# Two layers of graph attention: all products of the slots in four 64 by 64 tiles of TensorE

## The chip, the cores and the metric

The kernel runs on one core of a Trainium2 chip. The metric is the device time of one execution in microseconds. Shown are the median of three runs, and one further execution that the hardware profiler recorded.

## The reference, cut to what matters

Two layers on `x` of shape (8, 2048, 256), float32, with one adjacency matrix of 2048 by 2048 and four heads of 64.

```python
# layer 0: attention in chunks of 256 keys, each with its own softmax, summed over the chunks
q, k, v = (x @ Wq.T + bq, x @ Wk.T + bk, x @ Wv.T + bv)        # each split into 4 heads of 64
scores = clip(einsum('bhnd,bhjcd->bhnjc', q, kc) / 8, -10, 10)  # j: 8 chunks, c: 256 keys
scores = where(mask == 0, -10, scores)
ctx = einsum('bhnjc,bhjcd->bhnd', softmax(scores, -1), vc)
out = layernorm(ctx @ Wo.T + bo + x) * gamma + beta
x = layernorm(x + out)
# layer 1: graph attention
Wh = x @ W                                                      # 4 heads of 64
e = leaky_relu(s_src[:, :, None, :] + s_dst[:, None, :, :], 0.2)
alpha = softmax(where(adj != 0, e, -inf), axis=2)
x = layernorm(x + elu(einsum('bijh,bjhd->bihd', alpha, Wh)))
```

## The kernel before, in words

The eight batches follow one another. Layer 0 of batch b runs beside layer 1 of batch b - 1 (`lower`), so that the first batch has layer 0 alone and a last stretch has layer 1 alone. The order of the work is written out by hand: a manual schedule keeps every engine's program order, and tables give the step at which each side job is issued.

**Layer 0 runs in slots**, 64 per batch. A slot is 512 queries (`q`), a pair of heads (`hp`) and a chunk of 256 keys (`c`), in two tiles of 128 keys (`u`). In the loop over `s` (lines 934 to 999) the program issues, in this order: the slab of mask limits for slot s + 3 (`load_slab`); the side job of the table "ahead"; `normalize(s - 1)`; `scores(s + 1)`; side jobs "beside"; the first half of `product(s)`; the exponentials of slot s + 1 on ScalarE; a step of layer 1; the second half of `product(s)`; the jobs "behind".
- `scores` (L375) makes four products `ps` of 64 (one head's width) by 128 keys by 512 queries; the two heads of a pair lie in the upper and lower 64 partitions, so these are two row tiles, 64\*128. VectorE then clips and masks each `ps` of 128 by 1024 into `pr` (L396).
- `product` (L411) takes `pr` as weights, 128 keys by 64 queries, against `vaug`, 128 keys by 64 values and a one for the denominator. Outputs go to the upper or lower 64 partitions of `pc`, so these are two column tiles, 128\*64. ScalarE copies each `pc` to `raw` (L429).
- `normalize` takes the reciprocal (VectorE) and multiplies and adds on GpSimd.

**Layer 1 (`Layer1`)** works on units of a head and 1024 nodes (`BANKS = (8, 8)`), each over 16 tiles of 128 neighbours. `make` (L741, VectorE) forms a tile `e` of 128 by 1024 from a row `srow`, a column `gd` and a mask `et`; `use` (L763, TensorE) multiplies it with `waug` in two column tiles, 128\*64, summing a unit in two banks `pa`. Two tiles are made and used per slot; the ring of `e` has three buffers, and `make` is two tiles ahead.

**Side jobs.** `Between` does the output projection (`po`, L537), two layer norms, and layer 1's input product (`pw`, L581) of a group of 512 nodes; `Closing` does the last layer norm; `project` makes keys, queries (`pp`, L329) and values (`pv`, L345) for the next batch between slot 63 and slot 0 (the list `order`, L1028); `factors` (`fs`) makes layer 1's exponentials there. All of these use TensorE as 128\*128.

**PSUM**[...]: two pairs that `two_banks` gives out in turn (`psA`: `ps`, `pp`, `pv`, large `po` and `pw`), one `psC` for `pc`, two `psL` for `pa` and small things, and one `psM` for `po`, `pw` of few rows, `context` and `factors`.

A float32 matmul of the program stands in the trace as two pairs of LDWEIGHTS and MATMUL; these are called records below.

Of the kernel before, what the change touches and what calls it, by code (L numbers as in the profile page):

```python
# [8 lines left out]
F32 = mybir.dt.float32  # L9
# [13 lines left out]
def adj_resnorm_kernel(  # L23
# [35 lines left out]
    BANKS = (8, 8)  # L59
# [4 lines left out]
    QS = HP * NK  # L64
    SLOTS = NCH * QS
    UNITS = [(m, h) for m in range(len(BANKS)) for h in range(H)]
    FIRST = [sum(BANKS[:m]) for m in range(len(BANKS))]
    TILES = len(UNITS) * NT
    STEP = TILES // SLOTS
    LATE = 14  # L70
    WIDE = max(BANKS)
    JG = 2
    AHEAD_E = 3
    n_banks = WIDE // QT
    assert TILES == STEP * SLOTS and NT % JG == 0 and all(n == WIDE for n in BANKS)

# [5 lines left out]
    edges = ctx.enter_context(tc.tile_pool(name="edges", bufs=4))  # L82
# [5 lines left out]
    psM = ctx.enter_context(tc.tile_pool(name="psM", bufs=1, space=bass.MemoryType.PSUM))  # L88
# [30 lines left out]
    vaug = big.tile([P, NT, H, D1], F32, tag="vaug", name="vaug")  # L119

    clipD = [tc.dram_tile([P, NT, CH], I8, name=f"clipD{q}") for q in range(NCH)]
    edgeD = [tc.dram_tile([P, NT, n * P], U8, name=f"edgeD{m}") for m, n in enumerate(BANKS)]
# [36 lines left out]
    w1_sb = consts.tile([P, KC, F + 2 * H], F32, tag="w1_sb", name="w1_sb")  # L159
    nc.scalar.dma_start(out=w1_sb[:, :, :F], in_=w1.rearrange("(c p) f -> p c f", p=P))  # L160
# [10 lines left out]
    def finish_constants():  # L171
        for k, a_sb in enumerate(aa):
            for c in range(KC):
                wa = small.tile([P, F], F32, tag="ee", name="wa")
                nc.vector.tensor_mul(wa, w1_sb[:, c, :F], a_sb)
                nc.vector.tensor_reduce(
                    w1_sb[:, c, F + k * H : F + (k + 1) * H],
                    wa.rearrange("p (h d) -> p h d", h=H),
                    AX.X,
                    ALU.add,  # L180
                )


        pb0 = psM.tile([P, CH], F32, tag="psM", name="pb0")
# [22 lines left out]
    class Masks:  # L207
# [34 lines left out]
        def turn(self, t, m, ab):  # L242
# [11 lines left out]

            def stores():
                nc.sync.dma_start(
                    out=clipD[q][:, j0 : j0 + n, u * P : (u + 1) * P], in_=clip[:, :n]
                )
                nc.sync.dma_start(out=edgeD[mi][:, j0 : j0 + n, at : at + P], in_=edge[:, :n])
# [46 lines left out]
    def project(b, g):  # L306
# [34 lines left out]
        def values():  # L341
            pv = two_banks([P, QT, F], "pv")
            for u in range(QT):
                for kc in range(KC):
                    nc.tensor.matmul(  # L345
                        pv[:, u, :],
                        lhsT=st["xT"][:, kc, u * P : (u + 1) * P],
                        rhs=wv_sb[:, kc, :],
                        start=(kc == 0),
                        stop=(kc == KC - 1),  # L350
                    )
            nc.scalar.copy(
                vaug[:, QT * g : QT * (g + 1), :, :D],
                pv.rearrange("p t (h d) -> p t h d", h=H),
            )
# [9 lines left out]

    where = [(s // QS, s % QS // NK, s % NK) for s in range(SLOTS)]
    slab_of, probs, raws, accs = {}, {}, {}, {}

    def load_slab(s):
        q, hp, c = where[s]  # L370
        slab = slabs.tile([P, KT, CH], I8, tag="slab", name="slab")
        nc.sync.dma_start(out=slab, in_=clipD[q][:, KT * c : KT * (c + 1), :])
        slab_of[s] = slab

    def scores(s):  # L375
        q, hp, c = where[s]
        slab = slab_of.pop(s)
        cols = slice(q * CH, (q + 1) * CH)
        pss = []
        for u in range(KT):  # L380
            t = KT * c + u
            ps = two_banks([P, 2, CH], "ps")
            for k in range(2):
                rows = slice(k * D, (k + 1) * D)
                nc.tensor.matmul(  # L385
                    ps[:, k, :],
                    lhsT=kT[rows, hp, t * P : (t + 1) * P],
                    rhs=qT[rows, hp, cols],
                    start=True,
                    stop=True,  # L390
                )
            pss.append(ps)
# [17 lines left out]
    def product(s, k, alone):  # L410
        q, hp, c = where[s]  # L411
        if k == 0:
            raws[s] = small.tile([P, 2, QT, D1], F32, tag="raw", name="raw")

        if alone and k:
            pc = one_bank([P, QT, D1], "pc")
        else:
            pc = psC.tile([P, QT, D1], F32, tag="psC", name="pc")
        for i in range(QT):
            for u in range(KT):  # L420
                for z in range(2):
                    nc.tensor.matmul(  # L422
                        pc[z * D : (z + 1) * D, i, :],
                        lhsT=probs[s][u][:, k, i * P + z * D : i * P + (z + 1) * D],
                        rhs=vaug[:, KT * c + u, 2 * hp + k, :],
                        start=(u == 0),
                        stop=(u == KT - 1),
                    )
        nc.scalar.copy(raws[s][:, k], pc)  # L429

    def normalize(s):

        q, hp, c = where[s]
        raw = raws.pop(s)
        del probs[s]
        rd = small.tile([P, 2, QT, 1], F32, tag="rd", name="rd")
        nc.vector.reciprocal(rd, raw[:, :, :, D:D1])  # L437
        if c == 0:
            accs[q, hp] = small.tile([P, QT, 2, D], F32, tag="acc", name="acc")
        accv = accs[q, hp].rearrange("p t k d -> p k t d")  # L440
        part = accv
        if c:
            part = small.tile([P, 2, QT, D], F32, tag="part", name="part", bufs=1)
        nc.gpsimd.tensor_mul(part, raw[:, :, :, :D], rd.to_broadcast([P, 2, QT, D]))  # L444
        if c:
            nc.gpsimd.tensor_add(accv, accv, part)  # L446
# [3 lines left out]
    def send_context(b, q, hp):  # L450
        acc = accs.pop((q, hp))
        cols = slice(hp * P, (hp + 1) * P)
        nc.scalar.dma_start(
            out=by_node(ctxD, b, q)[:, :, cols], in_=acc.rearrange("p t k d -> p t (k d)")
        )

    def load_context(b, q, hp):
        t = small.tile([P, 1, CH], F32, tag="ctx", name="ctx", bufs=1)
        load_squares(t, ctxD[b, q * CH : (q + 1) * CH, hp * P : (hp + 1) * P])
        sums[q, hp] = t  # L460

    def turn_context(q, hp):

        nc.vector.transpose(qT[:, hp, q * CH : (q + 1) * CH], sums.pop((q, hp))[:, 0, :])  # L464

    def context(q, hp):
        acc = accs.pop((q, hp))
        pt = psM.tile([P, CH], F32, tag="psM", name="pt")
        for i in range(QT):
            nc.tensor.transpose(  # L470
                pt[:, i * P : (i + 1) * P], acc[:, i].rearrange("p k d -> p (k d)"), identf
            )
        nc.scalar.copy(qT[:, hp, q * CH : (q + 1) * CH], pt)
# [37 lines left out]
    class Between:  # L511
# [16 lines left out]
        def output(self, us):  # L528
            n = len(us)
            if n == QT:  # L530
                po = two_banks([P, QT, F], "po")
            else:
                po = psM.tile([P, 2, F], F32, tag="psM", name="po")
# [39 lines left out]
        def values(self, us):  # L573
            n, t = len(us), QT * self.g + us[0]
            if n == 1:
                pw = psM.tile([P, 1, CH], F32, tag="psM", name="pw")
            else:
                pw = two_banks([P, 2, CH], "pw")
            for k, u in enumerate(us):
                for c in range(KC):  # L580
                    nc.tensor.matmul(  # L581
                        pw[:, k, : F + 2 * H],
                        lhsT=self.x1T[:, c, u * P : (u + 1) * P],
                        rhs=w1_sb[:, c, :],
                        start=(c == 0),
                        stop=(c == KC - 1),
                    )
            nc.scalar.copy(
                self.waug[:, t : t + n, :, :D],
                pw[:, :, :F].rearrange("p k (h d) -> p k h d", h=H),  # L590
            )
            nc.scalar.copy(
                self.sd[:, :, t : t + n], pw[:, :, F : F + 2 * H].rearrange("p k x -> p x k")
            )
# [3 lines left out]
    AHEAD = {12: lambda o: o.load()}  # L598
    BESIDE = {
        1: [lambda o: o.bias()],  # L600
        4: [lambda o: o.add((0, 1))],
        5: [lambda o: o.add((2, 3)), lambda o: o.a.stats((0, 1))],
# [17 lines left out]
        4: [lambda o: o.add((0, 1))],  # L620
        5: [lambda o: o.add((2, 3))],
# [21 lines left out]
    def factors(b, sd, waug):  # L643
# [3 lines left out]
        s, d = sd[:, :H, :], sd[:, H:, :]  # L647
        top = small.tile([P, H], F32, tag="top", name="top")
        topb = top.unsqueeze(2).to_broadcast([P, H, NT])
        ed = small.tile([P, H, NT], F32, tag="ed", name="ed", bufs=1)  # L650
        gd = small.tile([P, H, NT], F32, tag="gd", name="gd")
        st = {}

        def most():
            nc.vector.tensor_reduce(top, d, AX.X, ALU.max)
            pt = psM.tile([P, CH], F32, tag="psM", name="pt")
            nc.tensor.transpose(pt[:H, :P], top, identf)
            st["most"] = small.tile([H, 1], F32, tag="most", name="most")
            nc.vector.tensor_reduce(st["most"], pt[:H, :P], AX.X, ALU.max)
# [446 lines left out]
```

## Time and profile before

| | us |
|---|---|
| median of 3 runs | 3774.59 (3774.26 to 3775.82) |
| profiled execution, its time | 3776.29 |
| profiled execution, its span | 3774.5 |
| TensorE matmul busy | 3664.0 (97% of the span) |
| VectorE busy | 3133.7 (83%) |
| ScalarE busy | 1988.0 (53%) |
| GpSimd busy | 1365.5 (36%) |

Engines are PE (TensorE's matmuls), PEld (its weight loads, which run beside matmuls), DVE (VectorE), ACT (ScalarE), POOL (GpSimd) and SPq (the queue of SyncE, from which most transfers are issued). A row of the profile names line, engine, operation, output and inputs, the shapes, the count, busy time and the mean of one in ns. The part after the last bar is the time that the engine sat idle before these instructions, and what ended it. "issue" means that the engine waited for nothing that the profile shows.

### The profile page before, as it was taken

The page shows a single profiled execution, that of the slowest core. Times are in us where ns is not written, and L with a number is a line of the kernel's source. Part 1 is how long each engine was busy: PE and PEld are TensorE (multiplying, and loading weights), DVE is VectorE, ACT ScalarE, POOL GpSimd, SP SyncE. Part 2 cuts the span into 40 slices and gives each one's busy share as a digit, 9 for nine tenths or more (in the row PEclk, how much of TensorE's full clock was granted, in tenths as well). Part 3 has the DMA queues.
Part 4 walks back from the last instruction along what each step waited for, and adds up shares of the span by engine and source line. Part 5 has one row for each costly group of instructions (what it writes and reads, how often), then busy time and mean ns, then how long its engine had stood idle before and what let it go on. Part 6 is the DMA issues. An engine that isn't in the chain of part 4 may idle for free.

```text
span 3774.5 us, 159666 instructions
## 1 busy us (share of the span) xinstructions
PE 3664.0 (97%) x72100; PEld 2741.3 (73%) x72100; DVE 3133.7 (83%) x4202; ACT 1988.0 (53%) x3665; POOL 1365.5 (36%) x1202
## 2 busy tenths in 40 slices
PE   9999999999999999999999999999999999999786
PEld 5656677776777777776777767777677777776676
DVE  5877489986999689895998959988699977988798
ACT  4666455555555555555555545555455555555322
POOL 1445234333433343333443324433334333334300
PEclk9999999999999999999999999999999999999998
DMA  6652333333333343333433334333433333433354
GB/s 163 152 117 69 78 98 109 105 75 112 106 108 105 86 119 102 104 93 88 133 97 98 100 89 135 109 100 78 113 107 107 105 80 112 115 97 84 95 154 128
DMA packets 672060, 398.46 MB, mean 106 GB/s; under 512 B 427280, under 2 KB 591504, under 8 KB 671376
## 3 DMA queue, kind: packets, MB, share of 16 engines
q1 hardware_dynamic: 621376, 354.54, 35.6%
q10 hardware_dynamic: 50000, 33.70, 2.8%
q8 instruction: 564, 9.24, 1.0%
q14 instruction: 120, 0.98, 0.1%
HBM read 331.22 MB, written 56.89 MB: 103 GB/s over the span
## 4 chain that ended last, share of the span: by engine, by line
PE 86%; DVE 5%; issue 3%; ACT 3%; DMA 1%; POOL 1%; SPq 0%; ACTq 0%; DVEq 0%; POOLq 0%
PE pc L422 26%; PE ps L385 24%; PE pa L763 22%; PE pp L329 5%; PE po L537 3%; PE pw L581 3%; PE pv L345 2%; DVE e L741 2%; ACT y L502 1%; DVE pr L396 1%; ACT pr L408 1%; DMA xp<-in_x_dram 0%; PE pm L246 0%; ACT qT L337 0%; SPq L279 0%
## 5 line engine op out<-in xcount | busy, mean ns | idle before, releaser
L396 DVE SCALAR_TENSOR_TENSOR pr<-ps,slab 128x1024 f32<-128x1024 f32 x1024 | 1194.3, 1207 | 211.1 <-PE ps L385 207.7
L422 PEld LDWEIGHTS pc<-vaug,pr 128*64 128x64 f32 x32768 | 1039.5, 138 | 406.4 <-issue 313.6
L741 DVE SCALAR_TENSOR_TENSOR e<-srow,gd,et 128x1024 f32<-128x1024 f32 x1024 | 1273.1, 1286 | 10.4 <-PE pa L763 5.8
L422 PE MATMUL pc<-vaug,pr 128*64 128x65 f32 x32768 | 1155.9, 224 | 14.3 <-ACT raw L429 7.7
L763 PE MATMUL pa<-waug,e 128*64 128x65 f32 x32768 | 1069.8, 224 | 41.0 <-DVE e L741 36.4
L763 PEld LDWEIGHTS pa<-waug,e 128*64 128x64 f32 x32768 | 1015.1, 139 | 60.1 <-DVE e L741 45.5
L408 ACT ACTIVATE pr<-pr 128x1024 f32<-128x1024 f32 x1024 | 1038.2, 1055 | 32.8 <-DVE pr L396 26.4
L385 PE MATMUL ps<-qT,kT 64*128 64x512 f32 x4096 | 1023.2, 616 | 3.5 <-DVE pr L396 2.9
L429 ACT COPY raw<-pc 128x260 f32<-128x260 f32 x1024 | 380.5, 372 | 1222.7 <-PE pc L422 1178.7
L444 POOL TENSOR_TENSOR part<-raw,rd 128x512 f32<-128x512 f32 x448 | 467.9, 1044 | 1407.5 <-DVE rd L437 1389.4
L446 POOL TENSOR_TENSOR acc<-acc,part 128x512 f32<-128x512 f32 x448 | 575.0, 1283 | 35.2
L385 PEld LDWEIGHTS ps<-qT,kT 64*128 64x128 f32 x4096 | 349.9, 186 | 326.6 <-issue 229.6
L437 DVE RECIPROCAL rd<-raw 128x8 f32<-128x8 f32 x512 | 100.8, 197 | 132.1 <-ACT raw L429 129.6
L444 POOL TENSOR_TENSOR acc<-raw,rd 128x512 f32<-128x512 f32 x64 | 66.7, 1043 | 339.3 <-DVE rd L437 339.3
L581 PE MATMUL pw<-w_sb,x1T 128*128 128x264 f32 x512 | 139.8, 409 | 6.1 <-DVE x1T L291 5.0
L795 ACT ACTIVATE sums<-sums,dn 128x64 f32<-128x64 f32 x512 | 134.0, 337 | 9.7 <-DVE dn L789 9.3
L497 POOL TENSOR_TENSOR rs_c<-rs_c,nhalf 128x4 f32<-128x4 f32 x32 | 54.0, 1687 | 223.8 <-DVE off_c L496 223.8
L537 PE MATMUL po<-wo_sb,qT 128*128 128x256 f32 x512 | 125.5, 390 | 3.1 <-DVE qT L464 2.8
L329 PE MATMUL pp<-xT,wk_sb 128*128 128x512 f32 x256 | 119.3, 609 | 7.9 <-ACT qT L337 6.6
L329 PE MATMUL pp<-xT,wq_sb 128*128 128x512 f32 x256 | 116.2, 597 | 0.0
L345 PE MATMUL pv<-wv_sb,xT 128*128 128x256 f32 x512 | 115.9, 379 | 0.0
L581 PEld LDWEIGHTS pw<-w_sb,x1T 128*128 128x128 f32 x512 | 92.4, 193 | 27.5 <-DVE x1T L291 5.3
(94 smaller groups left out, 1853.1 us busy)
## 6 DMA issues: line engine op xcount, KB each, us to landing
et<-edgeD SPq DMA_DIRECT2D x512, 256.0 KB, 3.1
slab<-clipD SPq DMA_DIRECT2D x512, 128.0 KB, 3.1
srow<-rowD SPq DMA_DIRECT2D x64, 512.0 KB, 5.0
xg<-in_x_dram SPq DMA_DIRECT2D x32, 512.0 KB, 5.3
x1D<-y ACTq DMA_DIRECT2D x32, 512.0 KB, 4.4
x1g<-x1D SPq DMA_DIRECT2D x32, 512.0 KB, 5.2
out_dram<-o SPq DMA_DIRECT2D x32, 512.0 KB, 3.3
ctxD<-acc ACTq DMA_DIRECT2D x56, 256.0 KB, 2.5
```

The source lines that it names most:

```text
L329: nc.tensor.matmul(pps[c], lhsT=w[:, kc, c * P : (c + 1) * P], rhs=st["xT"][:, kc, :], start=(kc == 0), stop=(kc == KC - 1),)
L385: nc.tensor.matmul(ps[:, k, :], lhsT=kT[rows, hp, t * P : (t + 1) * P], rhs=qT[rows, hp, cols], start=True, stop=True,)
L396: nc.vector.scalar_tensor_tensor(pr, pss[u], -CLIP, slab[:, u, :].unsqueeze(1).to_broadcast([P, 2, CH]), op0=ALU.max, op1=ALU.min,)
L408: nc.scalar.activation(pr, pr, AF.Exp, scale=0.125)
L422: nc.tensor.matmul(pc[z * D : (z + 1) * D, i, :], lhsT=probs[s][u][:, k, i * P + z * D : i * P + (z + 1) * D], rhs=vaug[:, KT * c + u, 2 * ...
L429: nc.scalar.copy(raws[s][:, k], pc)
L444: nc.gpsimd.tensor_mul(part, raw[:, :, :, :D], rd.to_broadcast([P, 2, QT, D]))
L446: nc.gpsimd.tensor_add(accv, accv, part)
L537: nc.tensor.matmul(po[:, k, :], lhsT=qT[:, c, t * P : (t + 1) * P], rhs=wo_sb[:, c, :], start=(c == 0), stop=(c == KC - 1),)
L581: nc.tensor.matmul(pw[:, k, : F + 2 * H], lhsT=self.x1T[:, c, u * P : (u + 1) * P], rhs=w1_sb[:, c, :], start=(c == 0), stop=(c == KC - 1),)
L741: nc.vector.scalar_tensor_tensor(e[:, :w], self.rows[n][:, :w], self.gd[:, h, j : j + 1], self.edge[k // JG][:, j % JG, :w], op0=ALU.max, ...
L763: nc.tensor.matmul(self.pa[i // QT][z * D : (z + 1) * D, i % QT, :], lhsT=e[:, i * P + z * D : i * P + (z + 1) * D], rhs=self.waug[:, j, h ...
```

## The change

All products within the slots take 64 partitions of input and 64 of output, so that four tiles of 64\*64 cover the array.

- **Slots.** A slot is now 256 queries (`qh`), all four heads and 256 keys. Head 2r + v stands for pair r and member v. `scores` multiplies 64 by 64 keys by 256 queries for each quarter (r, z): 16 matmuls instead of four. A `pr` tile keeps its 128 by 1024 elements; its partitions are (pair, 64 keys). `product` makes 64 matmuls instead of 32, of 64 keys by 64 queries by 65, into two banks `pcs`, one for each pair, and is issued in one piece ahead of the next exponentials; `keep` copies both banks to `raw` after these.
- **Layer 1** works on units of 6, 5 and 5 blocks of 128 nodes and two heads at once (partitions are (pair, 64 neighbours)), over 32 tiles. So a batch has 192 tiles `e` of 768 or 640 columns instead of 128 of 1024. A table `STEPS` gives three tiles for most slots, at times two or four; three are made ahead, in a ring that still has three buffers. Mask tiles `et` hold four of these (`JG = 4`) in three buffers instead of four.
- **Data that both pairs need** (`slab`, `et`) is loaded twice, once into each half of the partitions, by two transfers; `srow` comes in two halves.
- **`pv` and `pw`** are made for 64 nodes at a time, with outputs in either half: two column tiles, 128\*64.
- **PSUM**: `psC` takes two banks, `psM` is gone, and `po`, `pw`, `context` and `factors` take their tile from `two_banks`. So the adds that empty `po` move ahead of the next slot's scores (`WIDE_AHEAD`).
- `context`, `load_context` and `turn_context` work on 256 queries and all heads; the mask stores are split by halves; `ENDING` has other slot numbers.

```diff
-    BANKS = (8, 8)
+    BANKS = (6, 5, 5)
...
+    STEPS = (([3] * 10 + [2]) * 2 + [3] * 8 + [4] * 2) * 2
-    JG = 2
-    AHEAD_E = 3
+    JG = 4
+    AHEAD_E = 2
+    QUARTERS = [(r, z) for r in range(2) for z in range(2)]
+    HALF = [slice(0, D), slice(D, P)]
...
-    edges = ctx.enter_context(tc.tile_pool(name="edges", bufs=4))
+    edges = ctx.enter_context(tc.tile_pool(name="edges", bufs=3))
...
     def load_slab(s):
...
+        for rows in HALF:
+            nc.sync.dma_start(
+                out=slab[rows].rearrange("p u (g i) -> p (u g) i", g=2),
+                in_=clipD[q][:, qh, KG * c : KG * (c + 1), :],
+            )
...
     def scores(s):
...
-            for k in range(2):
-                rows = slice(k * D, (k + 1) * D)
-                nc.tensor.matmul(
-                    ps[:, k, :],
-                    lhsT=kT[rows, hp, t * P : (t + 1) * P],
-                    rhs=qT[rows, hp, cols],
+            for g in range(2):
+                j0 = (KG * c + 2 * u + g) * D
+                for r, z in QUARTERS:
+                    nc.tensor.matmul(
+                        ps[HALF[z], r, g * QH : (g + 1) * QH],
+                        lhsT=kT[HALF[r], z, j0 : j0 + D],
+                        rhs=qT[HALF[r], z, i0 : i0 + QH],
...
+    def product(s):
+        q, qh, c = where[s]
+        pcs = [psC.tile([P, 2, QU, D1], F32, tag=f"psC{r}", name="pc") for r in range(2)]
+        for v in range(2):
+            for i in range(QU):
+                for k in range(KG):
+                    for r, z in QUARTERS:
+                        at = k % 2 * QH + i * P + z * D
+                        nc.tensor.matmul(
+                            pcs[r][HALF[z], v, i, :],
+                            lhsT=probs[s][k // 2][HALF[r], v, at : at + D],
+                            rhs=vaug[HALF[r], KG * c + k, v, :],
...
     def use(self):
...
             for i in range(BANKS[m]):
-                for z in range(2):
+                for r, z in QUARTERS:
                     nc.tensor.matmul(
-                        self.pa[i // QT][z * D : (z + 1) * D, i % QT, :],
-                        lhsT=e[:, i * P + z * D : i * P + (z + 1) * D],
-                        rhs=self.waug[:, j, h, :],
+                        self.pa[r][HALF[z], i, :],
+                        lhsT=e[HALF[r], i * P + z * D : i * P + (z + 1) * D],
+                        rhs=self.waug[HALF[r], j, h, :],
...
-            product(s, 0, not lower)
+            pcs = product(s)
             if s + 1 < SLOTS:
                 for u in range(KT):
                     exps(s + 1, u)
+            keep(s, pcs)
             if lower:
                 if b + 1 < B or s < SLOTS - LATE:
                     lower.step()
             elif masks.left():
                 masks.step()
-            product(s, 1, not lower)
```

## The prediction, made before the changed kernel had run

> **What bounds the kernel now.** First the page's busy times and its chain of work that ended last.
>
> ```profile
> PE 3664.0 (97%) x72100; PEld 2741.3 (73%) x72100; DVE 3133.7 (83%) x4202; ACT 1988.0 (53%) x3665; POOL 1365.5 (36%) x1202
> PE 86%; DVE 5%; issue 3%; ACT 3%; DMA 1%; POOL 1%; SPq 0%; ACTq 0%; DVEq 0%; POOLq 0%
> ```
>
> TensorE sets the end; VectorE is not far behind. Next the chain in order of time over one slot of a late batch (start, length):
>
> ```profile
> 2006.40 1.92 PE ps L385 x8
> 2008.32 1.08 PE pc L422 x32
> 2009.40 1.87 PE pa L763 x64
> 2011.27 0.93 PE pc L422 x32
> ```
>
> A slot is 1.92 + 1.08 + 1.87 + 0.93 = 5.80 us, all TensorE. The second pc and pa run at 29.2 ns a record (1.87 / 64), and one of them, the first pc, takes 0.15 more for the same 32 records. The weight loads of that place show where this and ps lose time (start, length, idle before):
>
> ```profile
> 2006.87 0.19 PEld L385 LDWEIGHTS ps<-qT,kT 64*128 64x128 f32 x2 [0.23 <-issue]
> 2007.30 0.19 PEld L385 LDWEIGHTS ps<-qT,kT 64*128 64x128 f32 x2 [0.24 <-issue]
> 2008.25 1.01 PEld L422 LDWEIGHTS pc<-vaug,pr 128*64 128x64 f32 x32 [0.76 <-issue]
> 2009.17 1.95 PEld L763 LDWEIGHTS pa<-waug,e 128*64 128x64 f32 x64
> ```
>
> Inside ps a new pair starts every 0.43 us, so its eight records need 4 x 0.43 = 1.72 of their 1.92. From pc to pa, both 128\*64, loads run on without a gap; from ps (64\*128) to pc the loads stop with no engine to blame. Changing the tile shape thus costs 0.15 us into pc and 0.20 into ps, 0.35 a slot.
>
> Then busy times in the four stretches of 16 slots of batch 3 and the stretch to the next batch (window; length; PE, PEld, DVE, ACT, POOL):
>
> ```profile
> 1335.60:1429.10 93.50, 92.97 (x2057) 69.64 (x2056) 89.63 (x125) 55.49 (x92) 39.99 (x36) 1.00 0.44 132
> 1429.10:1525.80 96.70, 96.70 (x2198) 74.94 (x2194) 90.50 (x115) 51.13 (x92) 39.37 (x34) 1.00 0.35 101
> 1525.80:1626.80 101.00, 101.00 (x2212) 77.63 (x2210) 91.34 (x116) 54.82 (x104) 39.29 (x34) 1.00 0.37 102
> 1626.80:1722.00 95.20, 95.20 (x2076) 73.12 (x2074) 87.59 (x112) 54.09 (x104) 36.94 (x32) 1.00 0.37 99
> 1722.00:1785.20 63.20, 61.49 (x452) 41.49 (x450) 24.04 (x48) 28.39 (x60) 15.12 (x14) 1.00 0.36 73
> ```
>
> PE fills the slots, but DVE is within 4 to 10 us of it. The page's average of 83% hides that, because DVE rests between batches.
>
> [...]
>
> **The change part by part.**
>
> *Array time in slots: none.* Records halve in area and double in number, four at a time instead of two. ps: 32 of 256 columns, 32/4 x 0.215 = 1.72. pc: 128, in fours at pc's present 0.058 for a pair: 1.87. pa: three tiles of 5.33 x 8 = 43 records, 128 in all: 1.87. Sum 5.46 against 5.80 less 0.35. That four tiles run as two do is unproven; see the first rival.
>
> *Drains.* ps, pc and pa share a shape, so a plain slot saves 0.35. Where po or pw stands behind the slot (6 po and 8 pw among 63 slots, from the chain's pieces), its two drains stay and 0.15 goes: 49 x 0.35 + 14 x 0.15 = 19 us a batch.
>
> *VectorE.* Mask, exponent and norm work keep their elements. Tiles e: 192 of 683 columns on average instead of 128 of 1024, so only 64 fixed costs come on top. An e of 1024 takes 1286 ns and an h of 512 takes 733: 1.08 ns a column and 180 fixed. Back to back (eight e in 9.65 us at 3727) it is 1.206 each, leaving 0.10. I take 0.13: 2.1 us per 16 slots. Turning context in two pieces adds 0.1 each, 0.7 a batch.
>
> *What sets the slots then.* Per stretch, DVE after: 91.9, 92.8, 93.6, 89.7; PE after: 87.9, 91.5, 96.6, 91.2 (length less 16, 14, 10 and 9 drains of 0.35 and 0, 2, 6 and 6 of 0.15). The larger ones add up to 372.5 against 386.4. Two nearly full engines seldom mesh: make(k + 3) must wait until `use(k)` frees its buffer, and pc has one set of banks, emptied by `keep` behind two exponentials (2.0 us), which wait for pr. Behind a late pr on DVE stand the norm work and e; behind `keep` the next pc. Queue slack is 1 to 2 us. I charge 3.5 a batch: 376, a gain of 10.4, times 7 batches is 73. Bounds: 0 and 14 charged.
>
> *Batch 0* has no layer 1. 36 slots carry mask transposes (48 pieces less 12 at the start), which keep two drains: 27 x 0.35 + 36 x 0.15 = 15. But pc no longer alternates between two banks: ps end, pr 1.2, exponential 1.0, `keep` 0.7 fills nearly the whole slot of 3.6. I take half, 7; bounds 0 and 15.
>
> *Between batches.* pv in column tiles: 64 records of 128 columns, pairs at 0.109, 3.5 us as before (3.62); pw likewise. But pv and pw now differ in shape from pp and po: some five more drains, 0.9. `factors` share the turn with pp: q2 waits for vaug's copy (1.0), k3 for qT's (1.26), v3 for kT's (1.26), each less what lies between: 1.1 each, 3.3. Together 4.2, times 7 is 29. Bounds 5 and 45. In slots, po's add runs beside the first half of the next ps (0.86 against 0.68): nothing, and 0.3 x 48 if that cover goes; pw's two copies (0.6) likewise.
>
> *End.* Layer 1 alone is DVE's: 64 x 0.13 = 8 us, and 2 in the mixed steps before it: 10.
>
> *Transfers.* SP issues one more slab per slot and 256 more et, half a us each, in a queue whose issues now sum to 0.95 ms of the 3.77; et is asked for eight tiles ahead (14 us) and lands in 3.1. POOL's and ACT's queues carry the same bytes. Nothing; in the start, where the queue is full, 2 us for 96 more stores. Bounds 0 and 10.
>
> *Sum:* -73 - 7 + 29 + 10 + 2 = -39. From the span 3774.5 that is 3735.5. The profiled execution took 3776.29 with 1.8 around its span, the median of the runs is 3774.59, 1.7 lower: so 3735 for the median.
>
> **Rivals.** A measurement here tells 0.2% (7.5 us) from no change.
>
> *TensorE takes its records too slowly* (the slower side). A slot of 288 records must pass in 5.46, 18.9 ns each, and pc and pa in bursts of 256 at 14.6. No stretch in the trace is under 29. Against it: at a new ps two tiles' records start within 0.01 us (single records of the trace), so the array itself accepts them quickly; the instruction queue q8 would carry 18.5 MB at under 2% of the engines. [...]At 29.2: 8.4, +2.6 x 448 + 130 = about 5070. It decides from 19.6 ns, where slots eat the other gains. 0.20.
>
> *Four tiles don't quite overlap, or the drain was no drain but the wait of a first weight load*, which stays: then a slot stays near 5.8 and the additions of 41 count, 3815; with rounds of four at 66 ns instead of 58, 64 rounds x 0.008 = 0.5 a slot, +230 on the forecast: 3960. Against it: pc to pa shows no such first load. 0.12.
>
> *VectorE takes it all*: if an e costs 0.18 fixed and meshing costs 10 a batch, the slots' gain is about 5 a batch: 3775. The stretches' DVE column speaks for it. 0.13.
>
> **How the numbers follow.** Forecast 0.55: 3670 (no meshing loss, short waits) to 3767. Faster by over 0.2%: 0.55 and 0.02 of the third rival, 0.57. Within: 0.07 from the third. Slower: 0.04 of the third, 0.12 and 0.20, 0.36. The range runs from 3665 to 3960, leaving out the first rival. The forecast's own range is 3670 to 3767.
>
> **What would show it.** Right: slots of 5.5 to 5.7 us, no issue idle at pc's first load, DVE over 95% in the slots, 4 more us between batches. Wrong: pa records over 15 ns apart in the chain (first rival); 0.15 still lost into pc (second); PE waiting for pr or e in most slots (third).

## The result, and the profile after

| | before | after |
|---|---|---|
| median | 3775.2 us (4 runs) | 5113.56 us (5105.06 to 5118.52, 4 runs) |
| ratio | 1 | 1.354, interval 1.352 to 1.357 |
| span of the profiled execution | 3774.5 | 5108.9 |

The kernel became 35% slower: +1338 us, where 39 less were forecast. First the page of the changed kernel: busy times, granted clock, the instruction queue (packets, MB, share of the engines) and the chain of work that ended last.

```profile
PE 3878.2 (76%) x152996; PEld 3351.5 (66%) x152996; DVE 3265.6 (64%) x4778; ACT 2015.2 (39%) x3601; POOL 1326.3 (26%) x1186
...
PEclk9999999999999999999999999999999999999988
...
q8 instruction: 1195, 19.58, 1.6%
...
PE 70%; issue 22%; DVE 3%; ACT 2%; SPq 1%; DMA 1%; ACTq 0%; POOL 0%; DVEq 0%; POOLq 0%
```

No engine is full any more. TensorE fell from 97 to 76% and still leads the chain, and "issue", time in which it waited for nothing that the profile shows, went from 3 to 22% of the span. VectorE, which the forecast wanted at over 95% in the slots, has 64% of the span, and 67% in the 16 slots shown further down (95.86 of 142.1 us). The costliest groups say who waits:

```profile
L789 DVE SCALAR_TENSOR_TENSOR e<-srow,gd,et 128x640 f32<-128x640 f32 (+1 forms) x1536 | 1373.2, 930 | 1124.1 <-PE pa L811 1120.0
...
L811 PE MATMUL pa<-waug,e 64*64 64x65 f32 x65536 | 1250.6, 226 | 790.1 <-issue 759.9
...
L454 PE MATMUL pc<-vaug,pr 64*64 64x65 f32 x65536 | 1203.2, 220 | 275.8 <-issue 257.0
```

VectorE waits 1120 us for pa, and pa waits 760 us for nothing. Now batch 3: the first of its four stretches of 16 slots, and the way to batch 4 (window; length; PE, PEld, DVE, ACT, POOL; clock; DMA):

```profile
1748.10:1890.20 142.10, 102.00 (x4553) 91.89 (x4555) 95.86 (x140) 57.57 (x97) 36.68 (x34) 0.98 0.32 92
...
2295.70:2371.20 75.50, 65.22 (x1094) 47.06 (x1084) 26.61 (x54) 28.60 (x61) 16.82 (x13) 1.00 0.25 55
```

These 16 slots took 93.5 us before, with VectorE busy for 89.63 of them; now it is busy for 95.86 of 142.1. All four stretches take 547.6 us instead of 386.4. Slots of batches 1 to 7 lost 1101 us of the 1334 between the spans, batch 0 59, the ways between batches 82, the last stretch 90. What a slot looks like, the chain in order of time shows (start, length):

```profile
2761.05 2.16 PE ps L421 x32
2763.20 1.86 PE pc L454 x128
2765.07 0.19 PE pa L811 x14
2765.26 0.48 issue
2765.73 1.79 PE pa L811 x103
...
2773.35 1.71 PE pa L811 x118
2775.06 1.39 issue
2776.44 0.21 PE pa L811
2776.66 1.79 PE ps L421 x30
...
2784.28 1.73 PE ps L421 x32
```

Two things stand here. The array does what was forecast: 128 records of pc pass in 1.86 us (by the single records of the trace, a round of four every 58 ns, or 14.6 ns a record), and pc follows ps with no drain, the forecast's word for the 0.15 and 0.20 us lost in the kernel before where the tile shape changes. But the work comes in bursts. Between them are lumps of 0.4 to 2 us with nothing on TensorE, in the middle of ps, pc or pa. They do not belong to a product; they drift through the slot.

The single records of the trace say where the lumps sit. Within ps, pc and pa, and from one of them to the next, there are 1100 pauses of over 0.3 us from one start to the next, 1418 us together. Of these, 963, together 1325 us, end 1.1 to 1.8 us after a packet of q8, the queue that brings TensorE its instructions, has landed. Counted in weight loads and matmuls, nearly all of the 963 stand 256 instructions, or a multiple of that, after the one before (931 of 962 distances). That is the content of a packet: TensorE's 306,000 weight loads and matmuls came in 1195 packets, 256 to each, of 16.4 KB (19.58 MB / 1195). Such a packet is called a page here. The usual cycle, in medians: the page's transfer takes 1.02 us, TensorE resumes 1.40 us after it landed, and the next page's transfer starts 1.17 us after that: 3.6 us from page to page. What the 1.40 and the 1.17 consist of, the traces don't show. **TensorE runs out of instructions.** Over batch 3's slots, the transfers of the kernel after and of the kernel before:

```profile
q8 instruction: 140, 2.29, 1.7%
```

```profile
q8 instruction: 66, 1.08, 1.2%
```

That is a page each 547.6 / 140 = 3.9 us after, and each 386.4 / 66 = 5.9 us before, when TensorE was busy all the time. A plain slot of the changed kernel has 288 records of each kind, 576 instructions or 2.25 pages, and 2.25 times the median distance of page starts, 3.78, is 8.5 us. The median slot of batches 1 to 7 took 8.45.

### The profile page after: what moved, and what is told of

Read it like the earlier page. It is cut to its first block, busy times and chain, and to the rows that moved or that the text cites. A ratio compares the mean times of both kernels' runs of the same rounds, so it can differ in the third digit from the quotient of the medians.

```text
span 5108.9 us, 324751 instructions
## 1 busy us (share of the span) xinstructions
PE 3878.2 (76%) x152996; PEld 3351.5 (66%) x152996; DVE 3265.6 (64%) x4778; ACT 2015.2 (39%) x3601; POOL 1326.3 (26%) x1186
## 3 DMA queue, kind: packets, MB, share of 16 engines
q8 instruction: 1195, 19.58, 1.6%
## 4 chain that ended last, share of the span: by engine, by line
PE 70%; issue 22%; DVE 3%; ACT 2%; SPq 1%; DMA 1%; ACTq 0%; POOL 0%; DVEq 0%; POOLq 0%
PE pa L811 22%; PE pc L454 20%; PE ps L421 18%; PE pp L358 3%; PE pw L622 3%; PE po L579 2%; PE pv L375 2%; SPq L308 1%; ACT y L547 1%; DVE e L789 1%; ACT qT L366 0%; DMA clipD<-clip 0%; ACT pr L444 0%; DVE pr L432 0%; ACT vaug L382 0%
## 5 line engine op out<-in xcount | busy, mean ns | idle before, releaser
L789 DVE SCALAR_TENSOR_TENSOR e<-srow,gd,et 128x640 f32<-128x640 f32 (+1 forms) x1536 | 1373.2, 930 | 1124.1 <-PE pa L811 1120.0
L811 PE MATMUL pa<-waug,e 64*64 64x65 f32 x65536 | 1250.6, 226 | 790.1 <-issue 759.9
L811 PEld LDWEIGHTS pa<-waug,e 64*64 64x64 f32 x65536 | 1137.5, 140 | 864.3 <-issue 832.4
L454 PE MATMUL pc<-vaug,pr 64*64 64x65 f32 x65536 | 1203.2, 220 | 275.8 <-issue 257.0
L454 PEld LDWEIGHTS pc<-vaug,pr 64*64 64x64 f32 x65536 | 1164.5, 136 | 364.9 <-issue 321.6
L421 PE MATMUL ps<-qT,kT 64*64 64x256 f32 x16384 | 1119.9, 396 | 85.1 <-issue 67.7
L421 PEld LDWEIGHTS ps<-qT,kT 64*64 64x64 f32 x16384 | 746.4, 139 | 272.0 <-issue 141.5
L622 PE MATMUL pw<-w_sb,x1T 128*64 128x132 f32 x2048 | 144.4, 291 | 10.0 <-DVE x1T L320 6.0
L622 PEld LDWEIGHTS pw<-w_sb,x1T 128*64 128x64 f32 x2048 | 120.6, 143 | 24.8 <-issue 12.7
L375 PEld LDWEIGHTS pv<-wv_sb,xT 128*64 128x64 f32 x2048 | 111.5, 137 | 23.0 <-ACT kT L366 12.8
```

What stands on the lines that cost most here:

```text
L421: nc.tensor.matmul(ps[HALF[z], r, g * QH : (g + 1) * QH], lhsT=kT[HALF[r], z, j0 : j0 + D], rhs=qT[HALF[r], z, i0 : i0 + QH], start=True, ...
L454: nc.tensor.matmul(pcs[r][HALF[z], v, i, :], lhsT=probs[s][k // 2][HALF[r], v, at : at + D], rhs=vaug[HALF[r], KG * c + k, v, :], start=(k ...
L622: nc.tensor.matmul(pw[HALF[r], k, :W1], lhsT=self.x1T[:, c, node : node + D], rhs=w1_sb[:, c, r, :], start=(c == 0), stop=(c == KC - 1),)
L789: nc.vector.scalar_tensor_tensor(e[:, :w], self.rows[n][:, :w], self.gd[:, h, j : j + 1], self.edge[k // JG][:, j % JG, :w], op0=ALU.max, ...
L811: nc.tensor.matmul(self.pa[r][HALF[z], i, :], lhsT=e[HALF[r], i * P + z * D : i * P + (z + 1) * D], rhs=self.waug[HALF[r], j, h, :], start ...
```

## The experiments

Theory A: instructions reach TensorE no faster than a page in about 3.6 us, whatever they do. Rivals: the records' own time on the array; the reading and decoding of single instructions; pa's records in particular. "Wide" below means that one matmul takes 128 columns of `vaug` or `waug` at once where two took 65.

**1. Half as many records in pc and pa, with the array time kept.**

```diff
-        for v in range(2):
+        for v in range(1):
-                            rhs=vaug[HALF[r], KG * c + k, v, :],
+                            rhs=vaug[HALF[r], KG * c + k].rearrange("p v d -> p (v d)")[:, :P],
-            for i in range(BANKS[m]):
+            for i in range(3 if j % 2 else BANKS[m] // 2):
-                        rhs=self.waug[HALF[r], j, h, :],
+                        rhs=self.waug[HALF[r], j].rearrange("p v d -> p (v d)")[:, :P],
```

> The changed kernel with pc and pa in half as many matmuls, each of 128 moving columns instead of 65 (both members' values at once), still in four 64 by 64 tiles. TensorE's columns stay the same to 2%, its instructions fall from 306,000 to 175,000. Outputs of the left-out weights are not computed. Theory A (instructions arrive in pages of 256, one page at a time, about 3.6 us each): a slot has 320 instructions, 4.5 us of pages, so the array (5.25 us) or VectorE (about 5.1) sets it; the gaps called issue nearly vanish in the slots and the whole takes 3650 to 3850 us. Rival B (four tiles at once are slow in the array, or PSUM): same columns in the same tiles, so little changes, over 4700. Rival C (VectorE and TensorE wait for each other through the ring of e and the single set of pc): over 4700 as well.

Measured: 3828.6 us, 1.014 of before (1.0126 to 1.0157). From the page:

```profile
PE 3551.0 (93%) x87460; PEld 2916.6 (76%) x87460; DVE 3211.4 (84%) x4778; ACT 1989.9 (52%) x3697; POOL 1377.5 (36%) x1186
...
PE 37%; DVE 27%; issue 11%; ACT 9%; SPq 8%; DMA 8%; DVEq 0%; ACTq 0%; POOL 0%; POOLq 0%
```

1285 us are gone, with the tiles, the layout, VectorE's work and, within 2%, the array's columns as in the changed kernel. A round of four takes 108 ns instead of 58, for half as many rounds, so the array's time is nearly the same; pauses behind a page fall from 1325 us to 46. The chain is now shared by TensorE and VectorE, and batch 3's slots take 379 us. So four tiles and the missing drains do work; the number of records was the loss.

**2 and 3. Only one of the two products wide** (pa: the last two pairs of lines of the diff above; pc: the first two).

> The same for pa alone: 241,000 instructions; pa's left-out weights are not computed. Theory A: a slot has 448 instructions, 1.75 pages of 3.6 us are 6.3 us: about 4240 us, between the changed kernel and the one with both. Rival B or C: over 4700. If the cost sat in pa alone (its issue idle is three times that of pc), the time would fall to that of the kernel with both.

> The changed kernel with pc alone taken in 128 columns by half as many matmuls, pa left as it is (the products of the two heads of a pair are then not the right ones). It has the same number of TensorE instructions as the run with pa alone so, 241 thousand, 940 pages. Theory of instruction pages (one page of 256 instructions at a time, about 3.6 us each): the same time as that run within some 2%, 4250 to 4420, with TensorE's idle time again at the page boundaries. Rival, that the many short records of pa are what TensorE takes slowly, at their bank or behind e: pa's records are all there, so about as slow as the changed kernel, 4800 to 5100.

Measured: 4329.5 with pa wide (1.147, 1.145 to 1.149) and 4316.6 with pc wide (1.143, 1.141 to 1.145). Equal within 0.3%, though the one keeps pc's short records and the other pa's. Both rivals are out (over 4700, and 4800 to 5100); theory A's 4240 for the first was 90 too low, as a page took 4.0 us and not 3.6. Where only one product runs, its own count shows: batch 0's slots, without pa, take 369 us with pa wide and 338 with pc wide, and the last stretch, nearly all pa, 292 and 356. The cost goes by the count, not by the product. All kernels by their pages; the slots are those of batch 3:

| kernel | pages, all | pages in slots | slots, us | us a page | time, us |
|---|---|---|---|---|---|
| before | 564 | 66 | 386.4 | 5.9 | 3775 |
| both wide | 684 | 79 | 379.2 | 4.8 | 3829 |
| pc wide | 939 | 109 | 445.5 | 4.1 | 4317 |
| pa wide | 940 | 110 | 438.3 | 4.0 | 4330 |
| after | 1195 | 140 | 547.6 | 3.9 | 5114 |

In these runs the array and the other engines set the time at 4.8 us a page and more, and the page does at 4.1 and less.

**4. Do the kernel's own transfers slow the pages?** The slab and the mask tile are loaded once and kept.

```diff
+        if kept:
+            slab_of[s] = kept[0]
+            return
-        slab = slabs.tile([P, KT, CH], I8, tag="slab", name="slab")
+        slab = slabs.tile([P, KT, CH], I8, tag="slab", name="slab", bufs=1)
+        kept.append(slab)
...
+                if kept_edges:
+                    self.edge[k] = kept_edges[0]
+                    return
```

> The changed kernel with masks loaded once: one slab and one et serve everywhere, so some 1,800 transfers and about 190 of 338 MB are left out and the results are not the reference's; instructions of TensorE are as in the changed kernel. Theory A: a page's own transfer (0.89 to 1.38 us, median 1.02) goes to its lowest, 0.1 less per page of 1196, and perhaps as much again in its way there: 4850 to 5000. If TensorE's sequencer reads or decodes too slowly instead (rival D, some 13 ns for an instruction), nothing changes: 5113. If loads of masks were what VectorE and TensorE wait for, it falls below 4500.

Measured: 5038.05 (1.333, 1.331 to 1.336), 75 us less than the changed kernel and short of what theory A expected. A page's transfer stayed at 1.04 us (median) and its cycle at 3.77. Emptier queues did not bring pages sooner, so A was wrong on what lengthens a page. By its time alone this run doesn't decide between A and rival D, for which nothing was to change. Against D stand the single records: in bursts 256 instructions pass in 1.87 us (128 records at 14.6 ns), 7.3 ns each where D supposed some 13, and TensorE stops at the end of a page and goes on after a page has landed. 30 of the 75 us come from batch 0, whose slots fell from 365 to 335.

**5. Half the columns in as many matmuls.**

```diff
-        pcs = [psC.tile([P, 2, QU, D1], F32, tag=f"psC{r}", name="pc") for r in range(2)]
+        pcs = [psC.tile([P, 2, QU, D1 // 2 + 1], F32, tag=f"psC{r}", name="pc") for r in range(2)]
-                            rhs=vaug[HALF[r], KG * c + k, v, :],
+                            rhs=vaug[HALF[r], KG * c + k, v, D // 2 :],
-                        rhs=self.waug[HALF[r], j, h, :],
+                        rhs=self.waug[HALF[r], j, h, D // 2 :],
```

> The changed kernel with pc and pa multiplied in 33 columns instead of 65, in as many matmuls: the first half of each head's values is left out and filled with the other half by 1024 more copies on ScalarE, which has room (39% busy). The program keeps its instructions and its 1195 pages; the array has half the columns to pass in two of three products. Theory of instruction pages: nothing is gained, 5113 within 40 us. Rival, that the time of the records themselves on the array (its four tiles, their columns, their banks) sets the slots: [...]at least 150 us less, and up to 0.9 us a product, 800 us less.

Measured: 5280.4 (1.398, 1.395 to 1.402), 167 us *more* than the changed kernel: neither A's "within 40" nor the rival's "at least 150 us less". In bursts at full clock a round of four still takes 58 ns (median), with 33 columns as with 65. So this run did not shorten the array's time as it was meant to, and it doesn't decide on the rival; run 1 does, where the array's time stayed and the instructions were halved. The page shows what differs:

```profile
PEclk9899888888888988989888898898988988889755
...
L815 PE MATMUL pa<-waug,e 64*64 64x33 f32 x65536 | 1395.8, 240 | 651.7 <-issue 619.1
```

The granted clock is 0.86 in the mean instead of 0.967, and one record takes 240 ns where one of 65 columns took 226. By the clock records of the traces it is full or half: half for 28% of the span here, for 7% in the changed kernel. While the clock is full, page starts lie 3.77 us apart (median) in both kernels. Where part of the time between two starts is at half clock, it is 4.04 us here, 560 times, and 3.94 in the changed kernel, 156 times. An estimate from these medians, 560 x 0.27 - 156 x 0.17, gives 125 of the 167 us. So most of the loss lies in stretches of lowered clock. Which of the two brings the other, and why fewer columns go with a lower clock, stays open.

**6. The scores alone in quarters, in the kernel before.**

```diff
-                nc.tensor.matmul(
-                    ps[:, k, :],
-                    lhsT=kT[rows, hp, t * P : (t + 1) * P],
+                for z in range(2):
+                    nc.tensor.matmul(
+                        ps[z * D : (z + 1) * D, k, :],
+                        lhsT=kT[rows, hp, t * P + z * D : t * P + (z + 1) * D],
```

> The kernel before, with only the scores in four 64 by 64 tiles (64 keys by 512 queries), pc and pa as before in 128 by 64. 152,600 instructions, a slot has 288, so pages (4.1 us) are not the limit. If any change of tile shape drains TensorE, ps and pc still differ and the time is that of the kernel before within 0.5%. If only a change in the width of the tiles drains it, up to 0.35 us of each slot goes: down to 3620. If quarters are slow in themselves, ps takes longer: over 3800.

Measured: 3760.44 (0.9959, 0.9944 to 0.9974), faster than both kernels. The chain in order of time, and TensorE's loads (start, length, idle before):

```profile
2004.29 1.88 PE ps L386 x16
2006.16 1.08 PE pc L423 x32
```

```profile
2006.09 1.01 PEld L423 LDWEIGHTS pc<-vaug,pr 128*64 128x64 f32 x32 [0.81 <-issue]
```

ps goes from 1.92 to 1.88 (why, this run doesn't show), and pc keeps its 1.08, 0.15 over the 0.93 of the slot's second pc: from 64\*64 to 128\*64 the drain stays as from 64\*128. So a change in the rows of the tiles alone cost the same 0.15; it is gone in the changed kernel's chain, where ps and pc share a shape (1.86 us for 128 records, in rounds of four of 58 ns).

**7. The kernel before without psM**, which prices one term of the forecast alone.

```diff
-        pt = psM.tile([P, CH], F32, tag="psM", name="pt")
+        pt = two_banks([P, CH], "pt")
...
+    WIDE_AHEAD = {4: lambda o: o.add((0, 1)), 5: lambda o: o.add((2, 3))}
+    AHEAD = WIDE_AHEAD | {12: lambda o: o.load()}
```

> The kernel before with nothing changed but PSUM: psM is gone, and po, pw of few rows, context and factors take their tile from two_banks, as the changed kernel does, with the adds that empty po moved ahead of the scores. It tests one term of the forecast by itself, the waits for psA's turn between batches. The forecast had 3 x 1.1 us a boundary, 23 us in all, and nothing in the slots: 3798, range 3790 to 3806. If the 8 to 11 us a boundary that the wide kernel showed are all due to psM, it is 3775 + 7 x 9.5 = about 3840. If the waits are hidden by other work, it stays within 8 us of 3775. The theory of instruction pages expects nothing from it: TensorE's program keeps its 564 pages.

Measured: 3805.02 (1.0077, 1.0062 to 1.0092), +29. Between batches 67.1 us instead of 63.2, and the slots as before. The chain there has the waits that the forecast named (start, length):

```profile
879.97 1.02 ACT vaug L351
...
881.04 3.71 PE pp L328 x8
...
884.78 1.28 ACT qT L336 x2
...
890.42 0.69 ACT kT L336
```

TensorE stands three times until ScalarE has copied out the pair of banks whose turn it is.

**8, 9 and 10. What is left without the page limit.** The wide kernel of run 1 with the loads of run 4 left out; the same with four buffers for `e` (`ep` with `bufs=4`); and, as a control, the kernel before with the loads left out.

> The kernel with pc and pa in 128 columns (1.4% slower than before), and also with the slab and the mask tile et loaded once and kept, so every slot works with the same mask data: some 18 MB of transfers and their issues in SP's queue are left out. It asks what of the excess over the forecast, 94 us, is due to transfers. Theory T: the start of the program (batch 0 is 35 us longer than before) and part of the slots wait for SP's queue and for slabs: batch 0 goes back to about 310, and the whole to 3780 to 3795. Theory V: VectorE and the turns of PSUM make the excess, the transfers nothing, as the forecast said: 3815 to 3828.

> The run before this one with four buffers for e instead of three (the room comes from the mask tiles that are no longer loaded). It asks whether VectorE's make must wait until TensorE's use frees a buffer, the meshing for which the forecast charged 3.5 us a batch. Theory R, the ring binds: 3.5 to 10 us a batch come back, 25 to 70 us less than the run before this. Theory D, VectorE's own work binds and the ring has slack: within 8 us of it.

> The kernel before with the slab and the mask tile et loaded once and kept, so every slot works with the same mask data. It is the control for the run of the wide kernel with quiet loads, which was 52 us shorter than the wide kernel. If those 52 us are the price of the doubled transfers of the changed layout, the kernel before, whose slots are filled by TensorE, loses next to nothing by its own loads: 3765 to 3778. If half of them are what any kernel pays for these loads, it falls by about 26 us, to 3750.

Measured: 3776.35 (0.9999, 0.9991 to 1.0008), 3757.07 (0.995, 0.9935 to 0.9965) and 3776.76 (1.000, 0.9992 to 1.0009). The control is flat, so the 52 us between runs 1 and 8 are the price of the loads as the changed layout has them, 4 us more than theory T allowed. That it is their doubling, and not the larger mask tiles in fewer buffers, is likely but not shown: no run loads once in the new layout. 42 of the 52 lie in batch 0's slots (341 to 299; before 306), where SP's queue also stores the masks. In run 8's chain SP's queue and the transfers are down to 5% from 16:

```profile
PE 44%; DVE 30%; issue 12%; ACT 8%; DMA 3%; SPq 2%; POOL 0%; ACTq 0%; DVEq 0%; POOLq 0%
```

The ring of `e` holds back 19 us: between theories R and D, below R's lower end. 13 of them lie in the slots of batches 1 to 7, 1.9 a batch.

## Why the prediction was wrong, point by point

**The step that failed is the weighing of the first rival, and behind it "Transfers: nothing".** It held against that rival that "the instruction queue q8 would carry 18.5 MB at under 2% of the engines". The figure was good (19.58 MB, 1.6%) and the inference was not: the share of bandwidth said nothing about a queue that brought one page at a time, with 1.02 us of transfer in every 3.78 (medians). With 2.25 pages a slot, a slot of 5.46 us needs a page every 2.43 us; the changed kernel got one every 3.78 (median), and that cost the slots of batches 1 to 7 1101 us where 73 were to be won. The trace of before could warn of this, but not show the limit. Its page starts lie 5.74 us apart in the median and never under 3.3, so the pace that the forecast needed was nowhere in it. But TensorE itself took at least 3.73 us there for any 256 weight loads and matmuls in a row, so it never asked for pages much faster than they came.

**The first rival** had the direction and nearly the size (5070 for 29.2 ns a record, 8.4 us a slot; measured 5114) by another mechanism, and the nearness is luck: 29.2 ns was what a record takes on the array in the kernel before, which has nothing to do with pages. It looked for the loss in the single record; in the trace, records came 14.6 ns apart in bursts of four tiles. What is limited is the page: 3.78 us (median) for 256 instructions is 14.8 ns for each weight load or matmul, and a record needs one of each. Its sign to look for, pa's records over 15 ns apart, was met only in the mean.

**Array time and drains: right.** pc 1.86 us for 1.87 forecast, no pause from ps to pc, rounds of four every 58 ns. The second rival falls with this. ps took 1.73 in one of the lines shown and 2.16 in another, forecast 1.72.

With the page limit and the doubled loads out of the way (run 8), the other terms can be read one by one:

| term | forecast | run 8 against before |
|---|---|---|
| slots, batches 1 to 7 | -73 | -74 |
| batch 0 | -7 | -7 |
| between batches, 7 times | +29 | +55 |
| end | +10 | +22 |
| start | +2 | +3 |
| sum | -39 | -1 |

For slots and batch 0 the sums are as worked out, the 3.5 a batch for meshing included; for the slots that is in part luck. Batch 3's four stretches took 95.1, 97.0, 95.3 and 91.4 us in run 8, where the forecast had the busier engine at 91.9, 92.8, 96.6 and 91.2. The first two, with VectorE busy for 92.7 and 94.1 us, are longer than before, the third is shorter than forecast. That batch won 7.6 us where 10.4 were forecast, and batch 1 won 16. **Between batches was mis-sized.** The waits for psA's turn were 3.3 forecast and 3.9 measured (run 7). What the sum left out is a wait at its head. The chain of run 8 where batch 1 ends:

```profile
816.85 1.34 DVE e L799
...
818.23 0.90 PE pa L821 x24
...
821.20 1.30 ACT sums L856 x5
822.50 0.47 ACT waug L636
...
823.09 3.70 PE pp L358 x8
```

The first pp needs the banks that pw holds. pw's copy (`waug`) stands on ScalarE behind the closing of layer 1's last unit (`sums`, L856), and that behind the last e. pp starts 17.4 us after slot 63's scores start, against 14.6 before; over the seven ways it is 22 us more. Together with run 7's 27 that leaves some 6 of the 55 for the drains, forecast at 0.9 a way. The forecast had called pw's copies "nothing" without asking what is ahead of them on ScalarE.

**End: mis-sized, by e's cost there.** The groups of the last stretch (length 267.1 before, 289.6 in run 8), first before, then run 8:

```profile
L741 DVE SCALAR_TENSOR_TENSOR e<-srow,gd,et 128x1024 f32<-128x1024 f32 x154 | 188.6, 1285 | 5.9 <-PE pa L763 5.8
```

```profile
L799 DVE SCALAR_TENSOR_TENSOR e<-srow,gd,et 128x640 f32<-128x640 f32 x168 | 143.4, 921 | 7.7 <-PE pa L821 7.4
L799 DVE SCALAR_TENSOR_TENSOR e<-srow,gd,et 128x768 f32<-128x768 f32 x64 | 60.9, 1012 | 0.8 <-PE pa L821 0.7
```

As many columns in 232 pieces instead of 154 cost 204.3 - 188.6 = 15.7 us more, 0.20 each, where 0.13 was taken from between 0.10 and 0.18. Over the whole program it is 0.15 (1349.8 us against 1273.1, in 512 more pieces), so the 0.13 was near; why a piece costs more in the last stretch stays open. VectorE's idle time grew by 7 as well.

**Transfers: 2 forecast with a bound of 10; 52 measured**, apart from the pages. The issues of the doubled loads had been summed over the whole span, where there is room (0.95 ms of the 3.77). In batch 0's slots, where SP's queue stood waiting for only 92 of 341 us in run 1 (205 of 306 before), the loads cost 42.

**Third rival, VectorE takes it all:** with the pages out of the way the kernel would land there, at 3776 in run 8, but by the between and end terms. In batch 3's slots VectorE was busy for 363 of 379 us there, 96%, and 368 were forecast.

## What to carry to other kernels

Before splitting matmuls into smaller tiles, count the instructions of a stage, not only their time on the array: weight loads and matmuls of TensorE together, divided by 256, times some 3.8 us (what a page took in the changed kernel, 3.78 in the median), should stay below the stage's length. A float32 matmul is four instructions in these traces, 59 ns at that pace, so the short matmuls in four tiles at once, 29 ns for four instructions in bursts, outran their own program. For a queue that fetches one piece at a time, read the distance between its pieces in the trace, not its share of the bandwidth. Price a move of PSUM tiles by what stands ahead of the emptying copy on its engine (22 us of the 55 between batches in run 8), and added loads by the stage in which their queue is fullest (batch 0, 42 of the 52 us).

## What the runs showed of the hardware that was not expected

- Instruction pages of TensorE came one at a time, in medians of the changed kernel: transfer 1.02 us, 1.40 until TensorE resumed, 1.17 until the next transfer; starting no closer than 3.2 us in any of these traces, with much other traffic (the changed kernel, 1.02 us a transfer) or little (run 4, 1.04).
- In bursts at full clock TensorE started a record every 14.6 ns in four tiles of 64\*64, as quickly with 33 columns (run 5) as with 65 (the changed kernel); with 128 columns (run 1), every 27 ns.
- Going from 64\*64 to 128\*64 (run 6) left the same 0.15 us before pc as going from 64\*128 (before): 1.08 us instead of 0.93 in both.
- With half the columns in as many matmuls (run 5), the granted clock fell from 0.967 to 0.86 in the mean: at half clock for 28% of the span instead of 7%.
